# Attention with a mixture of experts: the value matmuls of a group's mixed and half tiles in one burst

## The chip, the core and the metric

The kernel runs on one core of a Trainium2 chip. The metric is the device time of one execution in microseconds. A profile of one execution stands beside the runs. TensorE (PE in the profile) multiplies matrices, and its weight loads are listed apart as PEld. VectorE is DVE, ScalarE is ACT, GpSimd is POOL and SyncE is SP.

## The reference

The kernel computes one transformer block in float32 on an x of 8 sequences, 512 tokens and 128 features. Cut to what matters:

```
xn  = layernorm(x)
q, k, v = split(xn @ W1 + b1)          # 16 heads of 8
w   = softmax(causal(q k^T / sqrt(8)))
att = (w v) @ Wp + bp
moe = shared_ffn(xn) + sum over the top 2 of 8 experts of weight * ffn_e(xn)
      # ffn(x) = (silu(x @ gate^T) * (x @ up^T)) @ down^T, 352 hidden features
out = x + att + moe
```

## The kernel before

**Groups, tiles and steps.** The attention is cut into 32 groups: 8 sequences, four groups of four heads each. A group's scores lie with the keys on the partitions and the queries along the row. What causality leaves of a head's 4 x 4 blocks is packed into five tiles of 1,024 columns, and each tile is one *step* of the main loop, 160 steps in all. Steps 0 and 1 of a group take the two *wide* tiles (keys 0 to 127, 512 queries for each of two heads). Steps 2 and 3 take the *mixed* tiles (two heads each: keys 128 to 255 with 384 queries, and keys 384 to 511 with 128). Step 4 takes the *half* tile (keys 256 to 383, 256 queries, all four heads).

**What a step does.** `weigh` fills a PSUM tile scT with scores (L321) and has ScalarE write its exponential into an SBUF tile pT (L442), of which there are four buffers. From step 40 on, GpSimd then sets to zero what causality forbids (L450). Before that a further matmul does it (L325).

**Peak scores.** The softmax needs each row's maximum, and `look` works on these some eleven tiles ahead. TensorE writes scores with the queries on the partitions into two PSUM banks, sc_diag and sc_left (L364). VectorE reduces them to peaks (L393, and L399 for a group's last). Before that `prepare` has ScalarE put the mask into sc_diag by a cast (L352), so the sc_diag matmuls of a step wait for the cast of the step before, and the cast waits for VectorE to have read the bank. Once a group, `shift_parts` makes the shifts out of the maxima on VectorE (L407 to L416). Two steps after the last of these looks, TensorE transposes the result (mT_ps, L422), VectorE copies it (L424) and SyncE carries it into the rows of q (L429).

**Experts beside it.** Between these, each step computes a third of a pair of expert blocks in `chunk`: gate and up products gu (L671, one PSUM buffer), tanh on ScalarE (th, L676), and two products on VectorE, the second of which is h (L678) and frees gu. `down` multiplies h back (y, L698; o on ScalarE, L704), and `turn_slots` turns the next tokens (s_ps, L642; sT, L657). These come up in the order y, y, s_ps, one a step. Every fourth group the projections of the next sequence's q and k come in too (qk_ps, L238, in steps 3 and 4). ScalarE moves these to rest (L245) and splits them (L246, L252), and VectorE takes the differences (L247, L253). The tiles y, s_ps, qk_ps and mT_ps share two PSUM buffers.

**The values.** `attend` (L465) multiplies pT by the values of its heads, which give 9 of 32 columns each. Four heads thus lie side by side as four strips of 32 columns of the array, and TensorE runs them at the same time. In the trace these are the matmuls `128*32`. One PSUM bank, av, collects two groups. Then ScalarE copies it to o_sb (L490), and sums are divided by the softmax's denominators. Each call of attend is kept in the list `late` and issued in the step after, behind that step's scores, peak scores and gu. So a group has three bursts of strips: the wide tiles in step 2, the mixed tiles in step 4 and the half tile in step 0 of the next group.

**Order.** The order on TensorE, VectorE, ScalarE and SyncE is that of the program. It is written out by hand, and nothing reorders it. GpSimd alone is placed by a scheduler.

Of the kernel before, what the change touches and what calls it, by code (L numbers as in the profile page):

```python
# [26 lines left out]
B, S, E = 8, 512, 128  # L27
# [3 lines left out]
NG = H // 4  # L31
# [33 lines left out]
def attn_moe_kernel(  # L65
# [140 lines left out]
    def pool(name, bufs, **kw):  # L206
        return ctx.enter_context(tc.tile_pool(name=name, bufs=bufs, **kw))
# [84 lines left out]
    def fetch(u, h0=0, h1=HH):  # L292

        b, half = divmod(u, 2)
        heads = slice(half * HH + h0, half * HH + h1)
        rows_q, rows_k = in_dram[b]
        for r in range(3):
            nc.sync.dma_start(qs[u % NU][24 * r : 24 * r + 24, h0:h1], rows_q[:, heads])
        for r in range(3):
            d = nc.sync.dma_start(  # L300
                ks[u % NU][24 * r : 24 * r + 24, h0:h1], rows_k[8 * r : 8 * r + 24, heads]
            )
        return d.ins
# [45 lines left out]
    def prepare(n, i):  # L349

        if i < 4:
            nc.scalar.copy(  # L352
                diag_ps.rearrange("p (b k) -> p b k", k=P),
                mask_q.unsqueeze(1).to_broadcast([P, NC, P]),
            )
        ahead.append(i)
# [81 lines left out]
    def weigh(n, kind, j, on_pool):  # L438

        ps = fill(n, kind, j, on_pool)  # L440
        pT = pr.tile([P, 2, S], F32, name="pT")
        last_exp[:] = [nc.scalar.activation(pT, ps, AF.Exp, scale=D**-0.5).ins]  # L442
        if on_pool:
            if kind == "half":
                diagonals = [pT.rearrange("p t (u k) -> p (t u) k", u=2)[:, :, :P]]
            else:
                diagonals = [pT[:, :, :P]] + ([pT[:, :, 3 * P :]] if kind == "mixed" else [])
            with tc.issue_after(sent[-1]):
                for d in diagonals:
                    nc.gpsimd.affine_select(  # L450
                        out=d, in_=d, pattern=[[0, d.shape[1]], [1, P]], compare_op=ALU.is_ge,
                        fill=0.0, base=0, channel_multiplier=-1,
                    )
        return pT
# [287 lines left out]
    def send_one(behind):  # L742

        if to_send:
            send(*to_send.pop(0), behind)
# [15 lines left out]
    def collect(b):  # L761

        r = later_pools["got"].tile([P, TOPK, NC, E], F32, name="r")
        for i in range(TOPK):
            d = nc.sync.dma_start(
                r[:, i].rearrange("p c e -> p (c e)"),
                results[ds(i * NT * P + b * S, S)].rearrange("(p c) e -> p (c e)", p=P),
            )
            for x_ in returned:
                tc.add_manual_dep(d.ins, x_.name, SYNC, reason="any pair may be in any block")  # L770
        got[b] = r
# [13 lines left out]
    late = []  # L785
# [3 lines left out]
    def due(step, f):  # L789
        ready.setdefault(step, []).append(f)  # L790
# [3 lines left out]
    def look(step, between=lambda: None):  # L794

        t = len(looked)
        if t >= total_steps:
            return lambda: None
        looked.append(step)
        n, i = divmod(t, NTILES)  # L800
        maxima(n, i, between)
        if i < NTILES - 1:
            return lambda: None
        if n == 0:
            return partial(shift_parts, n)
        if n < 4:
            return lambda: due(step + 1, partial(shift, n, shift_parts(n)))
        return lambda: first.setdefault(step + 2, []).append(partial(shift, n, shift_parts(n)))

    def side(step, most):  # L810

        for f in ready.pop(step, []):
            then(step, f())
        for _ in range(most):
            if aside:
                aside.pop(0)()
# [8 lines left out]
    def begin(step):  # L825
        for f in first.pop(step, []):
            more = f()
            if more is not None:
                more()
# [126 lines left out]
    def warm(k):  # L956

        ps = gu_ps.tile([P, NT * NE], F32, tag="gu", name="warm_ps")
        zero = none[:, :NT].rearrange("p t e -> p (t e)")
        for i in range(k):  # L960
            nc.tensor.matmul(ps, lhsT=zero[:, :P], rhs=zero, start=True, stop=True)
# [114 lines left out]
    def some_routing():  # L1076
        if not done_routing and next(routing, "end") == "end":
            done_routing.append(True)
            early.close()
            for name, bufs in (("wexp", 3 * MB), ("inp", 3), ("goes", 4)):  # L1080
                later_pools[name] = for_routed.enter_context(tc.tile_pool(name=name, bufs=bufs))
# [72 lines left out]
    def some_chunks(step, last):  # L1154
        for _ in range(max(chunks.get(step, 0) - 1, 0) if last else min(chunks.get(step, 0), 1)):
            extra()
# [42 lines left out]
    for n in range(B * NG):  # L1199
        b, g = divmod(n, NG)  # L1200
        waiting = []
        for i, (kind, j) in enumerate(TILES):
            step = n * NTILES + i
            begin(step)
            if step in fetches:
                fetch(fetches[step])
            on_pool = BUSY <= step < total_steps - 3
            waiting.append((kind, j, weigh(n, kind, j, on_pool)))

            if step - 1 in MORE:  # L1210
                some_chunks(step, False)
                parts_then = look(step)
            else:
                parts_then = look(step)
                some_chunks(step, False)
            if step in light:
                warm(5)
            parts_then()
            if step not in MORE and len(looked) < total_steps:
                prepare(*divmod(len(looked), NTILES))  # L1220
            some_routing()
            send_one(last_exp[0])
            for f in late:
                f()
            late = []
            if i == 1 and n % 2 == 0:
                av = av_ps.tile([P, S], F32, name="av")
            if i in (1, 3, 4):
                late = [partial(attend, n, waiting, av)]
                waiting = []  # L1230
            side(step, 2)
            some_chunks(step, True)
            send_one((last_gate or last_exp)[0])
            last_gate.clear()
            if step in MORE:
                look(step)()
            if len(stored) == NB // MB:
                if not all_back:
                    for_routed.close()
                    later_pools["got"] = pool("got", 6)  # L1240
                all_back.append(step)
            for _ in range(2 if len(all_back) > 1 else 0):
                if to_collect:
                    at_b = to_collect.pop(0)
                    collect(at_b)
                    at_ = all_back[0] + 3 + at_b
                    if at_b < B - 1:
                        for i_ in range(TOPK):
                            due(min(at_, total_steps), partial(add_up, at_b, i_))
                        due(min(max(at_ + 1, last_shift), total_steps), partial(store, at_b))  # L1250
        if n == B * NG - 1:
            continue
        if n % 2:
            late.append(partial(evacuate, n, av))
            due(step + 2, partial(divide, n))
        if g == NG - 1:
            due(step + 3, partial(turn, b))
            due(step + 4, partial(join, b))
# [80 lines left out]
```

## Time and profile before

| | |
|---|---|
| time, median of 3 runs | 585.21 us (584.29 to 586.15) |
| the profiled execution's own time | 585.24 us |
| its span, first to last instruction | 583.5 us |
| granted TensorE clock | 0.991 |
| busy: PE, PEld, DVE, ACT, POOL | 555.0, 409.0, 453.8, 375.9, 235.8 us |
| value matmuls (L465) | 1,024, busy 90.0 us |
| exponentials (L442) | 160, 164.0 us |

A line of a group of instructions gives the line of the kernel, the engine, the operation, the tile written and the tiles read, the shapes, the count, the busy time, the mean duration, and the idle time of the engine before it with what ended it. A line of the timeline begins with the start in microseconds from the first instruction and a duration. Neighbours of one kind are merged, and their number stands at the end. What stands in brackets is the idle time before it and what it waited for. The ends of matmuls are modelled, so the starts are what can be relied on for TensorE. A line of waits gives the waiting instruction, what it waited for, the microseconds in total, the times, and the longest. A line of a stretch gives its bounds, its length, the busy time of PE, PEld, DVE, ACT and POOL with the counts, the granted clock, the DMA share and GB/s.

### The profile page before, as it was taken

To read this page: it belongs to the slowest core of one execution; us is meant where nothing else is said; L and a number is where in the kernel's file an instruction comes from. 1 tells how busy PE (TensorE), PEld (TensorE's weight loads), DVE (VectorE), ACT (ScalarE), POOL (GpSimd) and SP (SyncE) were. 2 spreads that over 40 slices of the span, in tenths; PEclk is the share of its full clock that TensorE was granted. 3 is DMA by queue.
4 is the path that set the end of the run, shared out by engine and by line. 5 is a ranking of instruction groups with operands and counts; after the bars stand their busy time and mean duration, and the time that the engine had idled before them with its cause. 6 is when DMAs were issued, how large, how long until landed. Compare 5 with 4: busy or idle time off the path is not lost.

```text
span 583.5 us, 13669 instructions
## 1 busy us (share of the span) xinstructions
PE 555.0 (95%) x4809; PEld 409.0 (70%) x4809; DVE 453.8 (78%) x1199; ACT 375.9 (64%) x665; POOL 235.8 (40%) x362
## 2 busy tenths in 40 slices
PE   7989899999999999999999999999999999999995
PEld 4655576667776877777777777777777677777663
DVE  6688868878788877787887778887787787888657
ACT  5734554565557676686677767786667766676653
POOL 9521345544663134333443324433434243443430
PEclk9898899999999999999999999999999999999999
DMA  7745244143243785739685785849577575844057
GB/s 215 231 111 225 95 116 116 43 130 94 71 101 125 208 229 165 219 100 244 203 226 166 224 212 159 214 150 242 185 209 214 163 197 197 214 149 155 8 174 260
DMA packets 52380, 98.60 MB, mean 169 GB/s; under 512 B 10070, under 2 KB 35546, under 8 KB 50152
## 3 DMA queue, kind: packets, MB, share of 16 engines
q1 hardware_dynamic: 45960, 83.72, 50.2%
q0 software_dynamic: 5360, 13.80, 6.8%
q8 instruction: 38, 0.62, 0.5%
q10 hardware_dynamic: 992, 0.21, 0.2%
q14 instruction: 30, 0.25, 0.2%
HBM read 73.43 MB, written 24.40 MB: 168 GB/s over the span
## 4 chain that ended last, share of the span: by engine, by line
PE 79%; DVE 7%; ACT 6%; DMA 2%; POOL 2%; issue 2%; SPq 1%; DVEq 0%; POOLq 0%; ACTq 0%
PE gu L671 23%; PE av L465 13%; PE y L698 12%; PE scT L321 10%; PE sc_diag L364 6%; PE sc_left L364 5%; ACT sc_diag L352 2%; DVE peaks L393 2%; PE qk_ps L238 1%; PE s_ps L642 1%; ACT th L676 1%; DMA w<-in_w_exp_dram 1%; DMA ks<-dk 1%; DVE x_sb L776 1%; PE p_ps L539 1%
## 5 line engine op out<-in xcount | busy, mean ns | idle before, releaser
L442 ACT ACTIVATE pT<-scT 128x1024 f32<-128x1024 f32 x160 | 164.0, 1025 | 58.9 <-PE scT L325 39.7
L682 POOL DMA_INDIRECT results<-o,goes x72 | 72.4, 1005 | 131.2 <-ACT o L704 105.8
L671 PE MATMUL gu<-sT,w 128*128 128x128 f32 x864 | 116.6, 277 | 0.7 <-DVE row_max L408 0.4
L450 POOL TENSOR_SCALAR_AFFINE_SELECT pT<-pT 128x256 f32<-128x256 f32 (+1 forms) x163 | 71.4, 457 | 110.6 <-ACT pT L442 110.6
L671 PEld LDWEIGHTS gu<-sT,w 128*128 128x128 f32 x864 | 108.3, 191 | 5.3 <-PE sc_diag L364 2.3
L393 DVE TENSOR_REDUCE peaks<-sc_diag 128x4 f32<-128x512 f32 x128 | 87.8, 686 | 29.5 <-PE sc_diag L364 25.8
L321 PE MATMUL scT<-qs,ks 75*128 75x384 bf16 (+3 forms) x512 | 102.1, 300 | 1.3 <-ACT pT L442 1.2
L676 ACT ACTIVATE th<-gu 128x256 f32<-128x256 f32 x156 | 59.9, 384 | 48.2 <-PE gu L671 47.4
L465 PE MATMUL av<-pT,v_ext 128*32 128x512 f32 (+3 forms) x1024 | 90.0, 446 | 0.2 <-ACT pT L442 0.2
L749 POOL DMA_INDIRECT slots<-rows_attT,slot x64 | 61.7, 963 | 68.7 <-ACT pT L442 24.6
L677 DVE SCALAR_TENSOR_TENSOR th<-th,gu 128x256 f32<-128x256 f32 x156 | 65.1, 417 | 31.2 <-ACT th L676 28.8
L364 PEld LDWEIGHTS <-qs 72*128 72x128 bf16 x896 | 64.5, 97 | 32.2 <-issue 13.4
L393 DVE TENSOR_REDUCE peaks<-sc_left 128x4 f32<-128x512 f32 x128 | 87.0, 679 | 0.0
L352 ACT CAST sc_diag<-mask_q 128x512 f32<-128x512 bf16 x115 | 68.0, 591 | 17.9 <-DVE peaks L393 11.0
L678 DVE TENSOR_TENSOR h<-gu,th 128x256 f32<-128x256 f32 x156 | 66.1, 424 | 5.4
L698 PEld LDWEIGHTS y<-w,h 128*128 128x128 f32 x432 | 54.4, 191 | 22.4 <-issue 10.4
L364 PE MATMUL sc_diag<-ks,qs 72*128 72x128 bf16 (+1 forms) x576 | 61.8, 225 | 7.1 <-ACT sc_diag L352 6.2
L698 PE MATMUL y<-w,h 128*128 128x128 f32 x432 | 64.1, 285 | 1.4 <-ACT v_ext L288 1.4
L364 PE MATMUL sc_left<-ks,qs 72*128 72x128 bf16 (+1 forms) x320 | 61.5, 274 | 2.2 <-DVE peaks L393 2.1
L321 PEld LDWEIGHTS <-ks 75*128 75x128 bf16 x512 | 46.2, 98 | 18.7 <-issue 7.5
L671 PE MATMUL gu<-xnT,ws_sb 128*128 128x256 f32 x192 | 51.5, 391 | 0.9 <-DVE h L678 0.9
L704 ACT ACTIVATE o<-y,s 128x128 f32<-128x128 f32 x72 | 26.4, 367 | 36.9 <-PE y L698 27.9
(178 smaller groups left out, 624.2 us busy)
## 6 DMA issues: line engine op xcount, KB each, us to landing
w<-in_w_exp_dram SPq DMA_DIRECT2D x72, 576.0 KB
qs<-dq SPq DMA_DIRECT2D x45, 192.0 KB
ks<-dk SPq DMA_DIRECT2D x45, 192.0 KB
slots<-empty POOLq DMA_DIRECT2D x6, 792.0 KB, 5.8
s<-slots SPq DMA_DIRECT2D x33, 132.0 KB
r<-results SPq DMA_DIRECT2D x16, 256.0 KB
dq<-parts SPq DMA_DIRECT2D x7, 384.0 KB
dk<-parts SPq DMA_DIRECT2D x7, 384.0 KB
```

Source lines behind the costliest of these rows:

```text
L321: nc.tensor.matmul(out_, lhsT=k[: QK + 3, ts(i, P)], rhs=q[: QK + 3, i * P :], start=True, stop=bare)
L352: nc.scalar.copy(diag_ps.rearrange("p (b k) -> p b k", k=P), mask_q.unsqueeze(1).to_broadcast([P, NC, P]),)
L364: nc.tensor.matmul(out_, lhsT=q[:QK, ts(c, P)], rhs=k[:QK, keys], start=start, stop=stop, skip_group_check=True,)
L393: nc.vector.tensor_reduce(peaks[:, i, 8 + 4 * t : 12 + 4 * t], banks[t].rearrange("p (b k) -> p b k", k=P), AX.X, ALU.max,)
L442: last_exp[:] = [nc.scalar.activation(pT, ps, AF.Exp, scale=D**-0.5).ins]
L450: nc.gpsimd.affine_select(out=d, in_=d, pattern=[[0, d.shape[1]], [1, P]], compare_op=ALU.is_ge, fill=0.0, base=0, channel_multiplier=-1,)
L465: nc.tensor.matmul(av[32 * jj : 32 * jj + 32, c * P :], lhsT=v_ext[b % NV][:, c, 4 * g + jj, :], rhs=weights, start=(n % 2 == 0 and c == 0 ...
L671: nc.tensor.matmul(gu[:, i, part], lhsT=w[c][:, ds(i * FP + f * P, P)], rhs=sT[:, part], start=True, stop=True,)
L676: nc.scalar.activation(th, gu[:, 0], AF.Tanh, scale=0.5)
L678: last_gate[:] = [nc.vector.tensor_tensor(h[:, f], gu[:, 1], th, ALU.mult).ins]
L682: d = nc.gpsimd.indirect_dma_start(results, bass.IndirectOffsetOnAxis(ap=goes_of[k][0][:, c : c + 1], axis=0), o, None, bounds_check=NP - ...
L698: nc.tensor.matmul(y, lhsT=h[:, f, ts(c, P)], rhs=w[c % len(w)][:, ds(2 * FP + f * P, P)], start=(f == 0), stop=(f == NF - 1),)
```

## The change

The wide tiles' values stay where they were. In all groups but the last, the mixed tiles' values are no longer issued in step 4. They are kept until the half tile is there, and are then issued with it in step 0 of the next group, mixed tiles first. The last group still issues its mixed tiles in its step 4 and the half tile after the loop. As `attend` takes tiles of one kind, the list of waiting tiles is now split by kind.

```
             late = []
             if i == 1 and n % 2 == 0:
                 av = av_ps.tile([P, S], F32, name="av")
-            if i in (1, 3, 4):
-                late = [partial(attend, n, waiting, av)]
+
+            if i in (1, 4) or i == 3 and n == B * NG - 1:
+                late = [
+                    partial(attend, n, some, av)
+                    for kind in ("wide", "mixed", "half")
+                    if (some := [w for w in waiting if w[0] == kind])
+                ]
                 waiting = []
```

## The prediction

> **What bounds the kernel now.** I read the page's busy times and chain first, then TensorE's waits, then the timeline over two groups in the steady part (282 to 324 us). Steps are counted in a group: 0 and 1 are the wide tiles, 2 and 3 the mixed, 4 the half tile.
>
> ```profile
> PE 555.0 (95%) x4809; PEld 409.0 (70%) x4809; DVE 453.8 (78%) x1199; ACT 375.9 (64%) x665; POOL 235.8 (40%) x362
> ...
> PE 79%; DVE 7%; ACT 6%; DMA 2%; POOL 2%; issue 2%; SPq 1%; DVEq 0%; POOLq 0%; ACTq 0%
> PE gu L671 23%; PE av L465 13%; PE y L698 12%; PE scT L321 10%; PE sc_diag L364 6%; PE sc_left L364 5%; ACT sc_diag L352 2%; DVE peaks L393 2%; PE qk_ps L238 1%; PE s_ps L642 1%; ACT th L676 1%; DMA w<-in_w_exp_dram 1%; DMA ks<-dk 1%; DVE x_sb L776 1%; PE p_ps L539 1%
> ```
>
> TensorE is the chain for 79% of the span, so time taken from its stream can reach the end. But 7% and 6% lie on VectorE and ScalarE, and TensorE's waits say where:
>
> ```profile
> PE sc_diag L364 <- ACT sc_diag L352: 6.2, 13, 2.2
> PE gu L671 <- DVE h L678: 0.9, 4, 0.3
> ```
>
> The peak scores wait for the cast that puts the mask into their bank (L352), the gate products for the product h (L678) that frees theirs. Both appear in steps without a burst of values; the change makes one more such step.
>
> **What a burst costs.** TensorE's stream in step 0 (a burst of the half tile), step 1 (none) and step 2 (wide), where starts count:
>
> ```profile
> 304.85 1.06 PE L671 MATMUL gu<-sT,w 128*128 128x128 f32 x8
> 305.83 0.64 PE L465 MATMUL av<-pT,v_ext 128*32 128x256 f32 x8
> 306.40 0.94 PE L698 MATMUL y<-w,h 128*128 128x128 f32 x6
> 307.17 0.60 PE L321 MATMUL scT<-qs,ks 75*128 75x512 bf16 x2
> 308.05 1.06 PE L671 MATMUL gu<-sT,w 128*128 128x128 f32 x8
> 308.94 0.83 PE L698 MATMUL y<-w,h 128*128 128x128 f32 x6
> 309.61 0.60 PE L321 MATMUL scT<-qs,ks 75*128 75x384 bf16 x4
> 311.64 1.07 PE L465 MATMUL av<-pT,v_ext 128*32 128x512 f32 x8
> 312.64 0.44 PE L642 MATMUL s_ps<-ident,s 128*128 128x128 f32 x2
> ```
>
> Eight gu take 0.98 us ahead of a burst (304.85 to 305.83) and 0.89 without one (308.05 to 308.94): entry 0.09. Six y take 0.77 after one (306.40 to 307.17), 0.67 otherwise: 0.10 for a weight load that no matmul covers; before s_ps it is 0.05. The burst with half the columns takes 0.57 (305.83 to 306.40), the whole one 1.00 (311.64 to 312.64): 0.43 per 256 columns, so 0.14 fixed. A burst of its own costs about 0.33 us (0.28 before s_ps) beyond its matmuls.
>
> The Trainium skill ("TensorEngine Tiling (Array Packing)", Key Properties) says that a change of tiling mode drains TensorE, without a price; "TensorE: Matmul & The Clock Gate" (Part 2, Step-by-step) gives about 128 cycles for a drain, 0.053 us at its 2.4 GHz. Two drains would make 0.11 a burst, an estimate. The row has three times that, since weights too are loaded uncovered. I take the row: by the page the most to be won is 31 x 0.11 = 3.3 us, by the row 31 x 0.33 = 10.2.
>
> **The change, part by part.** It touches 31 of 32 groups; the last keeps its burst in step 4.
> - Step 4 loses the mixed burst: 0.09 + 1.00 + 0.10 = 1.19 us of TensorE time (1.15 before s_ps).
> - Step 0 of the next group does mixed and half together: 1.00 + 0.57 - 0.14 = 1.43 for 0.57, so 0.86 more. The matmuls are the same. Net, if nothing waits: -0.33.
> - Nothing is added on SP, POOL, ScalarE or VectorE, and no transfer changes. The four pT buffers are all live in step 0; the next exp, into the first mixed tile's buffer, follows scores that stand behind the burst in TensorE's order: no new wait. POOL's masking ends well before (the half tile's at 286.85, its burst starts at 290.42), and the half tile now comes last. The copy of av to o_sb (L490, every second group) waits 0.86 longer, with o and exp behind it, but these wait for TensorE work that is behind the burst too. Cost 0.
>
> **What covers step 4.** The burst gave VectorE and ScalarE 1.19 us. A joint from step 4 to step 0:
>
> ```profile
> 285.27 0.16 DVE L407 TENSOR_REDUCE row_max<-peaks 128x4 f32<-128x16 f32 x1
> 286.51 1.07 PE L465 MATMUL av<-pT,v_ext 128*32 128x384 f32 x16
> 287.05 0.68 DVE L393 TENSOR_REDUCE peaks<-sc_diag 128x4 f32<-128x512 f32 x1
> 287.51 0.94 PE L698 MATMUL y<-w,h 128*128 128x128 f32 x6
> 287.76 0.59 ACT L352 CAST sc_diag<-mask_q 128x512 f32<-128x512 bf16 x1 [0.77 <-DVE peaks L393]
> 288.69 0.42 DVE L678 TENSOR_TENSOR h<-gu,th 128x256 f32<-128x256 f32 x1
> 288.99 0.39 PE L364 MATMUL sc_diag<-ks,qs 72*128 72x128 bf16 x4
> 289.43 1.06 PE L671 MATMUL gu<-sT,w 128*128 128x128 f32 x8
> ```
>
> Once a group the row maxima (L407 to L416) and, here, a few routing words stand on VectorE ahead of the peaks: these start at 287.05 though their scores were there by 285.6. Then come the cast (ends 288.35) and h (289.11). All this follows from work ahead of the burst; none of it gets earlier when the burst goes. So sc_diag, at 288.99, can move up 0.64 less the 0.05 that every stalled sc_diag keeps behind its cast; gu, at 289.43, only 0.32 less 0.10 to 0.15 (at 218.15 it came 0.15 after an h that ended at 218.00). Step 4 gives 0.17 to 0.22 of its 1.19, and a gu so delayed runs 0.07 longer (1.06 from start to the burst's start for 0.99). Here the change costs 0.86 - 0.17 + 0.07 = 0.76 us instead of saving 0.33. The stage's busy time says the same:
>
> ```profile
> 284.07:288.54 4.47, 4.17 (x43) 2.93 (x41) 4.03 (x15) 3.11 (x7) 1.33 (x3) 1.00 0.50 201
> ```
>
> VectorE (third, 4.03) cannot do this step in 4.47 - 1.19 = 3.28. The skill's "Perfetto Trace Analysis" (Identifying the Most-Contended Engine) would have the engine with the highest occupancy optimized first; that is PE at 95%, and would count the full -10.2. In this stage the 4.03 decides against it.
>
> Every fourth group has another cover. Where k is projected in step 4, the transpose of the maxima waits for the bank that ScalarE is still reading:
>
> ```profile
> 452.52 0.61 ACT L252 CAST parts<-rest 128x512 bf16<-128x512 f32 x1
> 453.79 0.69 ACT L245 ACTIVATE rest<-qk_ps,bk_sb 128x512 f32<-128x512 f32 x1 [0.65 <-PE qk_ps L238]
> 454.52 0.22 PE L422 MATMUL mT_ps<-ident,m_parts 128*48 128x128 bf16 x1 [0.56 <-ACT rest L245]
> ```
>
> With qk_ps earlier, L245 starts at 453.10, when L252 ends: 0.69 is won, not 1.19. Near 387 us L245 already follows L252, and nothing is.
>
> I read the slacks of cast, h and L245 at all 31 joints in this way:
> - 10 joints nearly free (slack of gu behind h about 1.1 or more, as 1.16 at 222 us): -0.33 to -0.04 each, sum -1.8.
> - 7 with 0.65 to 0.95 of slack at gu: sum +2.3.
> - 8 like 289 us (slack at gu 0.2 to 0.6): 0.5 to 0.87 each, sum +6.0.
> - 6 with a k projection (won: 0, 0.23, 0.65, 0.67, 0.69, and about 0.6 at the first, which was not resolved): sum +2.3.
>
> Together +8.8 us with 0.15 and 0.07 at gu, +7.5 with 0.10 and 0.05. I take +8.0. Step 0 gives nothing back: the stall of a short step 1 comes from its own gu, th and cast. Sum: the profiled execution took 585.24 (span 583.5 and 1.7 around it), which is the median of the runs, 585.21, within 0.03. 585.2 + 8.0 = **593.2 us**.
>
> **Rivals.**
> - *The burst's full saving arrives* (faster): VectorE's and ScalarE's work in step 4 closes up as TensorE does. Price: 31 x -0.33 = -10.2, 575.0 us. For it: PE is 95% busy and no wait on h is over 0.3. Against: 4.03 us in that step, and 13 waits on the cast. It turns where h and the cast end 0.7 us earlier than at 289 us. A joint breaks even when step 4 gives up 0.86. Chance 0.09.
> - *The floors are softer*: no 0.07 after a stall, 0.05 behind h, the k joints at full gain. Then the same slacks sum to +1.1, 586.3 us. For it: the smallest distance from h to gu in the trace is 0.05. Against: where gu is bound by h, the next burst comes 1.06 after it, not 0.99. Chance 0.12.
> - *The long step 0 brings a wait of its own*: the copy of av starts 0.86 later and the 0.59 us of it, in 15 groups, pushes exp and the cast of step 1 back until TensorE waits: 15 x 0.59 = 8.9 more, 602 us. For it: ScalarE is strictly in order there. Against: exp of step 1 also waits for scores behind the burst. Chance 0.12.
> - *The bursts do not join*: excluded, both are issued one after the other in TensorE's hand-written order.
>
> **Numbers.** Likeliest 0.67 (own range 589 to 597). A measurement of this kernel tells 0.3%, 1.76 us, from no change. The first rival is faster (0.09), the second half same, half slower (0.06 each), the rest slower: 0.85. Range 586.5 to 600: it leaves out the first rival, a little of the second, and half of the third.
>
> **What would show it.** In the profile after: a burst of 24 matmuls of 1.43 us in step 0 and none in step 4; PE's wait for h and the cast grown by 8 to 12 us in sum, at step 0; step 4 near 284 us some 0.2 shorter, step 0 some 0.9 longer; mT_ps waiting for rest at the k joints. Wrong if step 4 is shorter by 1.1 everywhere, if step 1 changes its length, or if DMA waits (0.4 us on w now) move by microseconds.

## The result, and the profile after

The changed kernel took 593.3 us (median of 4, 592.34 to 595.28) against 585.68 for the kernel before (584.29 to 587.49): a ratio of 1.0134, with a 95% interval of 1.0101 to 1.0167. It is slower by 7.6 us, and the forecast was 593.2. The profiled execution took 595.28 us, with a span of 593.6. Here and below, ratios and intervals are over the fast runs alone and medians over all runs, so a ratio need not be the quotient of two medians.

The page after, busy times and the shares of the chain that ended last:

```profile
PE 553.0 (93%) x4809; PEld 410.2 (69%) x4809; DVE 452.0 (76%) x1199; ACT 374.9 (63%) x665; POOL 236.1 (40%) x362
...
PE 71%; ACT 9%; DVE 8%; DMA 6%; POOL 2%; issue 2%; SPq 1%; POOLq 0%; ACTq 0%; DVEq 0%
```

The instructions are the same in number, and TensorE is busy 2.0 us less, but over a span that is 10 us longer. Its share of the chain falls from 79% to 71%. TensorE's waits after the change:

```profile
PE sc_diag L364 <- ACT sc_diag L352: 9.7, 20, 2.6
PE mT_ps L422 <- ACT rest L245: 4.9, 5, 1.3
...
PE gu L671 <- DVE mT L424: 2.0, 6, 0.8
PE gu L671 <- DVE h L678: 1.8, 7, 0.4
```

Before, these four were 6.2, 1.1, none and 0.9. The prediction shows the first and the last of them, and the second was

```profile
PE mT_ps L422 <- ACT rest L245: 1.1, 2, 0.6
```

They grew by 3.5 + 3.8 + 2.0 + 0.9 = 10.2 us. The joint that the prediction showed at 284 to 292 us, in the timeline after:

```profile
288.20 0.68 DVE L393 TENSOR_REDUCE peaks<-sc_diag 128x4 f32<-128x512 f32 x1
288.50 0.60 PE L321 MATMUL scT<-qs,ks 75*128 75x512 bf16 x2
288.92 0.59 ACT L352 CAST sc_diag<-mask_q 128x512 f32<-128x512 bf16 x1 [0.76 <-DVE peaks L393]
289.56 0.38 PE L364 MATMUL sc_diag<-ks,qs 72*128 72x128 bf16 x4 [0.45 <-ACT sc_diag L352]
289.84 0.42 DVE L678 TENSOR_TENSOR h<-gu,th 128x256 f32<-128x256 f32 x1
290.41 1.13 PE L671 MATMUL gu<-sT,w 128*128 128x128 f32 x8 [0.25 <-DVE mT L424]
291.47 1.50 PE L465 MATMUL av<-pT,v_ext 128*32 128x384 f32 x24
292.90 0.94 PE L698 MATMUL y<-w,h 128*128 128x128 f32 x6
```

One burst of 24 matmuls takes 1.43 us (291.47 to 292.90). Ahead of it TensorE waits twice, first for the cast and then behind h, which ends at 290.26. The gu starts 0.15 after that end and takes 1.06 to the burst. The view puts this wait down to mT (L424), the copy that VectorE ends last before it. But in "two_again" (a second trace of this kernel, see below) gu starts 0.10 or 0.15 after h at every joint from step 40 on where it waits, but for the last (0.05), with that copy in between or without it. So h is what it waits for. Steps 4 and 0 of this joint as stretches (the busy columns are PE, PEld, DVE, ACT, POOL):

```profile
285.23:288.50 3.27, 2.97 (x27) 2.44 (x24) 2.83 (x13) 2.46 (x5) 1.32 (x3) 1.00 0.59 213
288.50:293.68 5.18, 4.48 (x48) 2.90 (x48) 3.90 (x9) 3.26 (x6) 1.43 (x2) 1.00 0.06 17
```

Before, they were 4.47 and 3.22 us long. Step 4 is 1.20 shorter, step 0 is 1.96 longer, and the joint costs 0.77 more. VectorE's 4.03 us of step 4 now reach into step 0.

Below, a *joint* is a step 4 with the step 0 behind it, measured between the first score matmuls of the steps. Against before, the 31 joints sum to +8.2 us. The changed kernel was run again beside later experiments (run "two_again"), and there they sum to +8.2 too, out of a span longer by 8.0. The 2 us by which the first profiled span is longer come with single waits for a transfer, above all one step of group 17 that is 3.0 us longer than before (0.4 in "two_again"; the last section comes back to it). In all other steps from 40 to 150 of "two_again" the sum moves by less than 0.3 us.

### The profile page after: what moved, and what is told of

It reads as the page before. It is cut to its first block, busy times and chain, and to the rows that moved or that the text cites. A ratio compares the mean times of both kernels' runs of the same rounds, so it can differ in the third digit from the quotient of the medians.

```text
span 593.6 us, 13669 instructions
## 1 busy us (share of the span) xinstructions
PE 553.0 (93%) x4809; PEld 410.2 (69%) x4809; DVE 452.0 (76%) x1199; ACT 374.9 (63%) x665; POOL 236.1 (40%) x362
## 4 chain that ended last, share of the span: by engine, by line
PE 71%; ACT 9%; DVE 8%; DMA 6%; POOL 2%; issue 2%; SPq 1%; POOLq 0%; ACTq 0%; DVEq 0%
PE gu L671 21%; PE av L465 12%; PE y L698 11%; PE scT L321 9%; PE sc_diag L364 5%; PE sc_left L364 4%; DMA w<-in_w_exp_dram 3%; DMA ks<-dk 3%; ACT sc_diag L352 2%; DVE peaks L393 2%; ACT th L676 2%; ACT pT L442 1%; DVE th L677 1%; PE p_ps L539 1%; DVE h L678 1%
## 5 line engine op out<-in xcount | busy, mean ns | idle before, releaser
L671 PE MATMUL gu<-sT,w 128*128 128x128 f32 x864 | 117.8, 279 | 4.3 <-DMA w<-in_w_exp_dram 1.4
L393 DVE TENSOR_REDUCE peaks<-sc_diag 128x4 f32<-128x512 f32 x128 | 87.5, 684 | 38.9 <-PE sc_diag L364 33.7
L677 DVE SCALAR_TENSOR_TENSOR th<-th,gu 128x256 f32<-128x256 f32 x156 | 65.2, 418 | 34.3 <-ACT th L676 31.9
L393 DVE TENSOR_REDUCE peaks<-sc_left 128x4 f32<-128x512 f32 x128 | 86.9, 679 | 0.0
L465 PE MATMUL av<-pT,v_ext 128*32 128x512 f32 (+3 forms) x1024 | 84.1, 446 | 0.2 <-ACT pT L442 0.2
L321 PEld LDWEIGHTS <-ks 75*128 75x128 bf16 x512 | 46.3, 98 | 21.7 <-issue 10.5
```

Of the source, the lines that this page charges most:

```text
L321: nc.tensor.matmul(out_, lhsT=k[: QK + 3, ts(i, P)], rhs=q[: QK + 3, i * P :], start=True, stop=bare)
L393: nc.vector.tensor_reduce(peaks[:, i, 8 + 4 * t : 12 + 4 * t], banks[t].rearrange("p (b k) -> p b k", k=P), AX.X, ALU.max,)
L465: nc.tensor.matmul(av[32 * jj : 32 * jj + 32, c * P :], lhsT=v_ext[b % NV][:, c, 4 * g + jj, :], rhs=weights, start=(n % 2 == 0 and c == 0 ...
L671: nc.tensor.matmul(gu[:, i, part], lhsT=w[c][:, ds(i * FP + f * P, P)], rhs=sT[:, part], start=True, stop=True,)
```

## The experiments

The kernel before took 585.7 and 586.4 us in two of the four sessions, 594.3 and 594.5 in the other two. Two traces of one kernel from different sessions (the changed kernel with a light shift, below) differ by 8.0 us before step 40 (186.3 and 194.4) and by 0.5 from there to step 150. So times are compared within a session, and single steps from 40 on also across sessions.

**1. What a burst of its own costs** (extra_burst). The wide burst of step 2 is cut into two, and `later` issues the second part.

```
+            half = slice(part * 2 * P, (part + 1) * 2 * P)
             for jj, w in heads:
-                add(jj, 0, w)
+                nc.tensor.matmul(
+                    av[32 * jj : 32 * jj + 32, half], lhsT=v_ext[b % NV][:, 0, 4 * g + jj, :],
+                    rhs=w[:, half], start=(n % 2 == 0 and part == 0), stop=False,
...
             side(step, 2)
+            if i == 2:
+                later()
```

> From the kernel before: the wide tiles' burst of step 2 is cut by columns into two, the first 256 columns where the burst was, the other 256 behind that step's y or s_ps. Nothing else moves. It measures the price of a burst of its own in a step that has cover. By the row of the trace (0.09 to enter, 0.14 fixed, 0.10 for an uncovered weight load) 32 x 0.33 = +10.6 us, so 594 to 598. By an estimate of two drains alone, 32 x 0.11 = +3.5, about 589. If TensorE had room in step 2, no change.

Measured: 602.2 us against 594.3, a ratio of 1.013 (1.0065 to 1.0194): 7.9 us more, less than the 10.6 expected from 0.33. TensorE's stream in a step 2, first before, then in this run:

```profile
278.29 0.60 PE L321 MATMUL scT<-qs,ks 75*128 75x384 bf16 x4
280.31 1.07 PE L465 MATMUL av<-pT,v_ext 128*32 128x512 f32 x8
281.31 0.94 PE L698 MATMUL y<-w,h 128*128 128x128 f32 x6
282.08 0.60 PE L321 MATMUL scT<-qs,ks 75*128 75x384 bf16 x4
```

```profile
292.02 1.13 PE L676 MATMUL gu<-sT,w 128*128 128x128 f32 x8
293.08 0.64 PE L476 MATMUL av<-pT,v_ext 128*32 128x256 f32 x8
293.65 0.94 PE L703 MATMUL y<-w,h 128*128 128x128 f32 x6
294.52 0.64 PE L476 MATMUL av<-pT,v_ext 128*32 128x256 f32 x8
295.09 0.34 PE L321 MATMUL scT<-qs,ks 75*128 75x384 bf16 x1
```

The step, whose first scores are at 291.05 in this run, grew from 3.79 to 4.04 us, and from step 40 on almost every step 2 grew by 0.24: the entry (0.09) and the fixed part (2 x 0.57 - 1.00 = 0.14). The 0.10 for an uncovered weight load is not paid again, since what follows the second burst is a bf16 score and not y. So a burst costs 0.24 before scores (32 of them make 7.7, the time measured) and 0.33 before y. Four joints of the changed kernel show the second number, -0.33, and with the light shift below all ten free ones come within 0.09 of it. The prediction's estimate from two drains alone, 0.11, is out.

**2. The transpose of the maxima alone moved** (late_turn). One number: `step + 2` becomes `step + 4` for `shift`, with `shift_parts` left where it was.

> From the changed kernel (593.3): only the transpose of the maxima (mT_ps, its copy and transfers) moves, from the start of step 0 to the start of step 2, one and a half steps behind the burst. Theory (VectorE's row maxima make h and the cast late; the transpose's wait for the k projection is a second, smaller cause): the five k joints lose their wait and get back 0.5 to 1.2 us each, together about -4; the joints bound by h or the cast do not move; the transpose itself costs about as much in step 2 as in step 0. 588 to 591. Rival (the transpose waiting in the queue is the main cause): nearly all of the loss and the saving come back, 575 to 580.

Measured: 607.9 against 594.3 us (1.0219, 1.0191 to 1.0248), so the time was missed by far. The joints did what the theory says. The five with a k projection that had lost something got back 1.30, 1.30, 0.88, 1.24 and 1.30, and from step 40 on the others stayed within 0.1. But in step 2 the transpose cost 0.26 where y or s_ps came before it, and 0.8 and more where step 1 also divides the sums, since there it waits for a PSUM buffer. Steps 1 grew by 15.1 us in all, and one step with a wait of 3.7 us for expert weights grew by 5.9. The k joints' cause is shown. The expected saving went into the place that I had chosen for the transpose.

**3. VectorE's maxima out of step 4** (late_shift_two, late_shift_three, late_shift_apart, late_shift_put).

```
-    peaks = const.tile([P, 4, 17], F32, name="peaks")
+    peaks_of = []
+    for i in range(2):
+        t = const.tile([P, 4, 17], F32, name=f"peaks{i}")
...
+        peaks_of.append(t)
...
-        return lambda: first.setdefault(step + 2, []).append(partial(shift, n, shift_parts(n)))
+        return lambda: due(step + 2, lambda: late_shift(step + 4, n))
+    def late_shift(at_, n):
+        first.setdefault(at_, []).append(partial(shift, n, shift_parts(n)))
```

> From the changed kernel (593.3): the row maxima and shifts on VectorE (L407 to L416) move from between steps 3 and 4 to the end of step 0, the long step, with two peaks tiles in turn so that the next group's peaks do not overwrite them; the transpose follows in step 2. Theory: step 4 has no late VectorE work any more, the joints bound by h, the cast and the transpose come down to about -0.33 less what a short step waits for its own cast (0.1 to 0.2), so 576 to 580, under both kernels. Rival (the long burst in step 0 is itself the cost, by what waits behind it): 589 to 594, as VectorE's work in step 4 would not matter.

> From the kernel before (585.2): the same move of the row maxima and the transpose, with the three bursts left as they were. Theory: step 4 was covered by its burst, so VectorE's lateness cost little there; the transpose goes from step 0 into a place where TensorE partly waits anyway: 580 to 585. The difference to the run with two bursts is then the saving of the joined burst where it has cover, 4 to 9 us. Rival (two bursts save nothing in themselves): no difference between the two.

Measured: 617.6 us with two bursts (four runs, 608.2 to 623.3) and 615.2 with three (614.2 to 621.2), against 594.3. The two are not told apart, and both expectations failed as times. The joints with two bursts fell as expected: those at 0.77 to 0.79 by 1.2, the middle ones by 0.22 to 0.37, so that most stand at -0.43 or 0.02 against before, and 13.1 us in all. With three bursts most of them fell by 0.27, which is the transpose itself. So it is work on VectorE between steps 3 and 4 that makes the joints late. But steps 1 grew by 22 us and steps 2 by 12. The timeline of late_shift_two shows the first of two causes, at the end of a step 1 with v:

```profile
271.88 0.94 PE L703 MATMUL y<-w,h 128*128 128x128 f32 x6 [1.59 <-ACT v_ext L291]
272.86 0.37 ACT L709 ACTIVATE o<-y,s 128x128 f32<-128x128 f32 x1 [1.02 <-PE y L703]
273.27 0.22 PE L427 MATMUL mT_ps<-ident,m_parts 128*48 128x128 bf16 x1 [0.46 <-ACT o L709]
```

With one transpose more in this place, y waits for the buffer of v, and the transpose for the buffer that o reads. The second cause, late weights, stands at the head of TensorE's waits in the same run:

```profile
PE gu L676 <- DMA w<-in_w_exp_dram: 9.1, 5, 5.5
```

In late_shift_apart the transpose goes to step 3 where step 1 divides the sums:

> From the changed kernel: as in the run with the row maxima at the end of step 0 and two peaks tiles, but the transpose goes to the start of step 3 in the groups in which step 1 also divides the sums (there it had waited 0.8 to 2.6 us in step 2 for a PSUM buffer), and to the start of step 2 in the others. Theory: the joints come down as in that run (by 1.2 at the worst, 0.37 at the middle ones, 0.9 to 1.3 at the k joints) and the transpose costs 0.1 to 0.26 instead of 0.8 on average: 4 to 9 us under the kernel before. If the transpose's transfers then come too late for the next group's scores, or if step 4 has another cover to lose: at or above the kernel before.

Measured: 613.5 us against 586.4 (1.0416, 1.0306 to 1.0526). The profile is of an execution of 627.4 us, and the other three took 608.8 to 615.7, so its waits are larger than those behind the median. In it steps 1 grew by 8.3 only, but the waits for w rose:

```profile
PE gu L676 <- DMA w<-in_w_exp_dram: 20.5, 7, 7.4
```

SyncE's order is that of the program. In this trace the transfers of the maxima (L434) left at 360.70, with a load of weights (L621) behind them at 363.68, and TensorE's gu waited 5.2 us for weights, until 365.93. Which load that was, the profile does not tell. In late_shift_put these transfers are issued one step later:

> From the run with the row maxima at the end of step 0 and the transpose in step 2 (617 and 613 us with the transposes later still): only the three transfers of the maxima into q's rows (L429) are issued one step later than their transpose. Theory: in those runs SyncE's queue stood at these transfers, waiting for the transpose, and the loads of the expert weights behind them came late (TensorE waited 9 to 20 us for w, and its clock went down after it). With the transfers behind, the waits for w go down to a few us, and the time to 580 to 590. Rival (the loads are late for another cause, the chip's or the transfers' own): waits for w stay at 9 us or more and the time over 600.

Measured: two runs only, 606.7 us (the profiled one) and 616.8, against 594.5. The profile has waits for w of 5.1. Against late_shift_two, three steps 2 got back 1.1, 1.6 and 3.1 us, so the order of the queue is likely to have had a part in it. But both times stayed far over 590, and the one wait for w that is left was not explained. The expectation fails. What of the lost time lies in the PSUM buffers, what in the transfers and what in the clock (last section) stays open.

**4. Less work on VectorE, in the same places** (light_shift_two, light_shift_three). Nothing is moved here. Three VectorE instructions of a group are left out, and the parts 1 and 2 that they wrote are zero in the two tiles of `one_part`.

```
-        parts = at.tile([P, 3, 16], BF16, name="m_parts")
-        rest = at.tile([P, 16], F32, name="m_rest")
+        parts = one_part[n % 2]
         nc.vector.scalar_tensor_tensor(parts[:, 0], m, -2.0, m, ALU.mult, ALU.add)
-        nc.vector.scalar_tensor_tensor(rest, m, -1.0, parts[:, 0], ALU.mult, ALU.subtract)
-        nc.vector.scalar_tensor_tensor(parts[:, 1], rest, 2.0, rest, ALU.mult, ALU.subtract)
-        nc.vector.tensor_tensor(parts[:, 2], rest, parts[:, 1], ALU.subtract)
```

> The changed kernel itself, unaltered, beside the kernel before on the chip of the three runs below: +7 to +10 us over before, as on the first chip (+7.6). It is the reference for them.

> From the changed kernel: the shift of a row's scores is kept as one bf16 number instead of the sum of three (L414, L415 and L416 are left out, the other two parts are zero), so about 0.63 us less VectorE work a group stands between the steps 3 and 4; a shift cancels in the softmax, and no instruction moves. Theory: the joints bound by VectorE get back up to 0.63 us each: those at 0.75 to 0.9 come down to 0.1 to 0.3, those at 0.3 to 0.4 to about -0.25, the k joints and the free ones stay. About 8 to 9 us less than the changed kernel, within 1.5 us of the kernel before. Rival (the long burst and what waits behind it): no more than 1 us less.

> From the kernel before: the same three VectorE instructions left out, three bursts as they were. Theory: step 4 is covered by its burst, VectorE's lateness costs nothing there; 0 to 1.5 us less than before. Rival (VectorE's work bounds the kernel anyway): 5 us less or more, and the same gain as in the run with two bursts.

Measured in one session, against 586.4 us before: the changed kernel 593.1 (1.0109, 1.0084 to 1.0134), with the light shift 582.3 (0.989, 0.9795 to 0.9986), and the kernel before with the light shift 585.7 (0.9977, 0.9948 to 1.0005). By the medians, leaving out the same three instructions is worth 10.8 us with two bursts (8 to 9 were expected) and 0.7 with three. And with the light shift the change itself no longer costs: the medians put it 3.5 us below three bursts, the joints 1.7. The first profile's joint at 285 us, in the timeline of light_shift_two:

```profile
285.03 0.17 DVE L417 SCALAR_TENSOR_TENSOR one_part<-row_max 128x16 bf16<-128x16 f32 x1
285.46 0.68 DVE L398 TENSOR_REDUCE peaks<-sc_diag 128x4 f32<-128x512 f32 x1
286.39 0.59 ACT L357 CAST sc_diag<-mask_q 128x512 f32<-128x512 bf16 x1
287.11 0.42 DVE L679 TENSOR_TENSOR h<-gu,th 128x256 f32<-128x256 f32 x1
287.28 0.39 PE L369 MATMUL sc_diag<-ks,qs 72*128 72x128 bf16 x4
287.72 0.97 PE L672 MATMUL gu<-sT,w 128*128 128x128 f32 x7
```

The cast now ends 0.30 ahead of sc_diag, and h 0.19 ahead of gu: no wait. In the two stretches of this joint step 4 is 3.28 us long, as in the changed kernel, and step 0 is 4.10 instead of 5.18:

```profile
283.56:286.84 3.28, 2.98 (x28) 2.45 (x25) 2.94 (x12) 2.81 (x6) 1.32 (x3) 1.00 0.80 323
286.84:290.94 4.10, 4.10 (x48) 2.90 (x47) 2.91 (x7) 2.91 (x6) 1.39 (x2) 1.00 0.09 25
```

All of the difference to the changed kernel lies in steps 0 (-10.5 us; every other step of a group sums to under 0.2). The k joints do not move. The long burst is untouched in this run, so it is not the cost. Not all of the 10.5 is the three instructions' own time (3 x 0.21 = 0.63 a joint): at six joints that fell by 1.04 to 1.08 a routing word (L645 or L649, small instructions of `turn_slots`) got faster too, by 0.41 to 0.45 (last section). That is about 2.6 us of the 10.5, and it is VectorE's time as well.

**5. The k joints as well** (light_again, light_shift_swap).

```
-        due(at_ + 1, partial(split_qk, b, 0))
         due(at_ + 1, partial(project_qk, b, 1))
+        due(at_ + 1, partial(split_qk, b, 0))
```

> The changed kernel with the shift in one bf16 part, once more, as the reference for the run below and for a firmer ratio: 3 to 6 us under the kernel before.

> From the changed kernel with the shift in one part: in step 4 of every fourth group the projection of k comes ahead of the second split of q, so ScalarE frees the PSUM bank of qk_ps (L245) ahead of its cast L252, and the transpose of the maxima waits for it 0.6 us less. Theory (at the k joints this wait took the saving): those five joints go from +0.86 and +0.12 to between +0.25 and -0.33, about 2 to 3 us less in all; nothing else moves. Rival (the k joints are bound by VectorE's split of q and k): no change, or up to 1 us more since the split comes later.

Measured against 594.5 us: 587.6 for the light shift (0.9868, 0.9821 to 0.9916; 3 to 6 us less were expected, and 6.9 came) and 586.1 with the swap (0.9867, 0.9816 to 0.9918). The two times don't tell the swap, but the joints do: the five fell by 0.45 to 0.52 each, 2.4 us in all, from +0.12 to -0.33 at three, from +0.55 to +0.03 and from +0.86 to +0.35. In the timeline of light_shift_swap the rest of k (L250) now comes ahead of the cast L257, and the transpose no longer stands behind that cast:

```profile
451.74 0.69 ACT L250 ACTIVATE rest<-qk_ps,bk_sb 128x512 f32<-128x512 f32 x1
452.48 0.22 PE L423 MATMUL mT_ps<-ident,one_part 128*48 128x128 bf16 x1 [0.56 <-DVE h L679]
452.98 0.61 ACT L257 CAST parts<-rest 128x512 bf16<-128x512 f32 x1
```

It still waits 0.56 us, and starts 0.05 behind the end of that rest (452.43), so rest is likely what still holds it. The view names h, which ends as it starts. Both versions are 1.3% faster than the kernel before, where the changed kernel was 1.1 to 1.3% slower in the sessions that had it. It was not run in this one.

## Why the prediction was right

The time was met to 0.1 us, and that closely by luck: +8.0 was taken between two workings of +8.8 and +7.5, misses of up to 0.9 in the classes cancel in part, and single runs lie 3 us apart. The working can be set against the joints, by the classes that the prediction made (us, against before):

| joints | forecast | changed kernel | two_again | with the light shift |
|---|---|---|---|---|
| 10 nearly free | -1.8 | -1.2 | -1.2 | -3.2 |
| 7 with 0.65 to 0.95 at gu | +2.3 | +2.1 | +2.1 | -0.6 |
| 8 with 0.2 to 0.6 at gu | +6.0 | +5.9 | +5.9 | +0.1 |
| 6 with a k projection | +2.3 | +1.4 | +1.4 | +1.4 |
| sum | +8.8, or +7.5; taken +8.0 | +8.2 | +8.2 | -2.3 |

- *What covers step 4*: right in mechanism and size. The example at 289 us was put at 0.76 and measured 0.77. The work that was named, L407 to L416 and the routing words on VectorE, is the cause: with three instructions of it gone, the joints fell by up to 1.08. But not at all joints. Those in groups 2, 29 and 30 (+0.42, +0.87 and +0.22) kept their cost with the light shift. In groups 29 and 30 there are no peak scores left, and in "two_again" gu waits for h through its own chain: gu at 556.90, th at 558.07, h until 559.36, the next gu at 559.51. There the burst covered that chain. No run tests it.
- *What a burst costs*: -0.33 net held at four joints, and with less VectorE work at all the free ones to 0.09; so the row, not the estimate from drains, was the right one to take. The price belongs to what follows the burst, as extra_burst shows with 0.24.
- *The k joints*: the mechanism was right, the size was off by 0.9. The first one, where I had not resolved the gain (0.6), gave all of it, -0.33 instead of +0.26. It is the joint at 53 us, whose step 4 projects q, and k follows in step 0; the next sequence's, at 113 us, is counted with the free ones (-0.25). Three of the others stand at 0.12, not at 0.17 to 0.21, since their step 4 gave 0.74 and not 0.65 to 0.69, and one at 0.55, not 0.63.
- One joint that I called free, in group 4, cost 0.35. Its step 4 has an extra look behind the burst, and I read only its gu.
- *Copy of av, SP, POOL*: cost nothing, as put. The rival in which the long step 0 brings a wait of its own falls: step 1 kept its length to 0.02 us in nearly every group from 40 on.
- *The marks to look for* were in part wrong. I wrote that step 4 near 284 us would be some 0.2 shorter and step 0 some 0.9 longer, and that a step 4 shorter by 1.1 everywhere would refute me. It is shorter by 1.15 to 1.20 in nearly all joints without k, and step 0 is longer by up to 1.99. The scores at the start of step 0 need neither cast nor h, so they moved up, and the wait stands behind them. The sum over the joint is what was predicted; the boundary was drawn in the wrong place. The waits for w rose to 1.4 us in the first profile, in one step, but are 0.4 in "two_again", so they are not the change's.
- *Where to look first*: the prediction has the Trainium skill's "Perfetto Trace Analysis" (Identifying the Most-Contended Engine) name TensorE, by its 95%. The same section says that the busy share of matmuls is no good measure of how close TensorE is to its limit, and takes the share of its peak arithmetic, which no view here gives, and the busy share of its weight loads. The second is 70% here, under VectorE's 78%. So the page does not simply name TensorE, and the -10.2 is not its forecast.

The rival of the full saving falls: only four joints have all of it. The rival of softer floors falls at the joints too: h to gu is 0.10 or 0.15, and at 290.41 the gu behind it takes 1.06. Its 586.3 us lies under the four runs.

## What to carry to other kernels

On an engine that is busy 95% of the time, a piece of work can still be the cover for others; before it is moved, read what the other engines finish just behind it, and give each joint its own slack. Here 1.19 us left a step that VectorE filled for 4.03 of 4.47 us, and it was three small instructions on VectorE, worth 10.8 us with the change and 0.7 without, that decided its worth. A new place for a small instruction has a price of its own, in buffers and in queues, that was larger here than what it freed.

## What the runs showed that was not expected

**Small VectorE instructions ran until a GpSimd instruction ended.** Two routing words, L645 and L649, over the kernel before (count, then shortest, median and longest in ns), and one of the long ones in its timeline:

```profile
L645 DVE TENSOR_TENSOR second<-s,expert_rank x36: 148/149/605, 192.1 to 534.6; 128x2 f32<-128x2 f32 x36
L649 DVE SCALAR_TENSOR_TENSOR goes<-second,s x36: 160/161/578, 192.2 to 534.7; 128x2 int32<-128x2 f32 x36
```

```profile
286.21 0.64 POOL L450 TENSOR_SCALAR_AFFINE_SELECT pT<-pT 128x512 f32<-128x512 f32 x1 [1.45 <-ACT pT L442]
286.26 0.60 DVE L645 TENSOR_TENSOR second<-s,expert_rank 128x2 f32<-128x2 f32 x1
```

Four of 36 L645 took about 0.60 us instead of 0.15. Each began 0.04 to 0.06 us after such a masking had begun, and ended with it to 0.02. Two more had begun 0.11 ahead of a masking and took 0.15, but then the L649 behind them began inside it and took 0.58 instead of 0.16. With one L413 and one L414, all eight of these small instructions that began inside a masking ran until it ended, to 0.04. All eight read their two operands from SBUF. The 17 L393 and 51 L677 that began inside one, and read a PSUM tile, took their usual time, and so did four L653 (COPY_PREDICATED). In light_shift_two L645 and L649 come earlier, miss the masking, and take 0.15 and 0.16 in all 36. That is why the worst joints got back 1.04 to 1.08 there and not the 0.63 that I had expected for three instructions. The two engines seem to share a path for such an instruction; that was not tried by itself.

**A wait of TensorE cost more than its length.** In the step of group 17 that is 3.0 us longer, TensorE waits 1.4 us for weights:

```profile
351.24 1.45 PE L671 MATMUL gu<-sT,w 128*128 128x128 f32 x6 [1.44 <-DMA w<-in_w_exp_dram]
352.62 1.94 PE L465 MATMUL av<-pT,v_ext 128*32 128x512 f32 x8
```

```profile
350.00:352.00 2.00, 0.76 (x4) 0.76 (x5) 0.77 (x2) 0.04 (x1) 0.77 (x2) 0.87 1.02 320
352.00:354.00 2.00, 2.00 (x12) 0.60 (x10) 0.82 (x2) 0.38 (x1) 0.00 (x0) 0.50 0.73 283
```

The granted clock is 0.50 from 352 to 354 us, behind the wait, and the burst takes 1.94 instead of 1.07. In "two_again" the wait in the same place is 0.4, the clock stays at 1.00, and the burst takes 1.07. In late_shift_apart, behind a wait of 5.2, the clock is 0.52 over 6 us; its matmuls, the same in number, are busy 567.2 us in all against 553.0. So here a wait of 1.4 us cost 3.0. No run here was made to test what lowers the clock.
